# A three-pass state-space, attention and feed-forward kernel: areas, start-up loads and six splits rearranged at the borders of its passes

## The chip, the cores and the metric

The kernel runs on one core of one Trainium2 chip. A core has five engines that work from instruction queues of their own, each in order: TensorE (PE, matrix products into PSUM), VectorE (DVE), ScalarE (ACT), GpSimd (POOL) and SyncE (SP, which here only issues DMAs). They share an on-chip memory (SBUF) and meet through semaphores; DMA engines move data between SBUF and device memory.

The metric is device time in microseconds (us). Before the change it is 9731.19 us, the median of three runs (9729.94 to 9732.88).

## The reference, cut to what matters

The input is an image batch of 8 x 64 x 64 x 96 in float32. The layer is computed in three stages, each with a residual sum:

```
# layer 0: group norm, then a selective scan in four directions
xin, z = split(group_norm(x) @ in_proj_w.T)            # 96 -> 192 + 192
xc     = silu(depthwise_conv3x3(xin) + conv_b)          # 192 channels, 64 x 64
xs     = [xc by rows, xc by columns, and both reversed] # K = 4 directions, length 4096
dts, B, C = split(x_proj_weight[k] @ xs[k])             # 6 + 16 + 16 rows
delta  = softplus(dt_projs_weight[k] @ dts + dt_projs_bias[k])
h      = h * exp(delta * A) + (delta * u) * B           # step by step, 16 states a channel
y      = sum_n(h * C) + D * u
out    = (layer_norm(y of 4 directions summed) * gamma + beta) * silu(z) @ out_proj_w.T
x      = x + out
# layer 1: attention without a softmax, on the 4096 tokens of an image
t = t + (q k^T / sqrt(16)) v @ Wff + bff                # of layer_norm(t), 6 heads
# feed-forward in float8 products with float16 sums
t = t + W2(relu(W1(layer_norm(t))))
```

The inner state has 192 channels, 16 states for each, 4 directions, 8 images and 4096 steps. Almost all of the time is in the scan over these.

## The kernel before, in words

**Three passes.** `pass1` (line 295) makes the group norm, the in-projection, the 3 x 3 convolution and silu, writes the convolved channels `u` to device memory by rows and by columns (`u_d`), and makes the x-projections (`xd_d`: dts, B and C in rows). `pass2` (line 569) runs the selective scan. `pass3` (line 961) adds up the four directions, does the layer norm and gate, out-projection, attention and feed-forward, and writes the output.

**The order of work is planned.** In each pass, work is written as small generators ("units") that yield before each step what engine it needs, an estimated cost and what must have been done. `weave` (line 169) simulates the engines with these estimates and issues the steps in the order that comes out; so a changed buffer, cost or condition can reorder instructions on an engine. `InOrder` (line 85) issues each instruction through one helper, and pins the order on that engine, which is why nearly all instructions of the profile show line 93. `Slots` (line 132) stands for buffers taken in turn, the next one only when the one that has been out longest is free; `Buffers` (line 151) for buffers of which the first free one is taken.

**Pass 1** handles the images in four pairs. 192 channels of two images are three blocks of 128 partitions, in the order (0, 2, 1): `convolution(pair, c)` (line 468) does nine taps on VectorE over a padded image `xpad` of 4096 elements a partition (one `tensor_scalar`, eight `scalar_tensor_tensor`), silu on ScalarE in two halves, four copies on ScalarE that turn rows into columns (`ut`, 1024 elements each) with two or three stores after each, and a store of `u` itself. Then `x_projection` (line 518), in pieces of 512 columns, and `split` (line 265).

**A split** makes three bfloat16 parts of float32 rows, so that later products can be done in bfloat16: one load `bq` from `xd_d`, a cast on ScalarE, a subtraction on GpSimd, a second cast, a second subtraction, and two stores. An image has two row orders (orientations) with three splits each: two for B (`b_d`) and one for dt (`dt_d`). `LATE = 5` (line 59): images 0 to 4 are split in pass 1, images 5 to 7 in pass 2 among the scans (`late_split`, line 722). `LATE_X = 7`: image 7's x-projections are late as well.

**Pass 2** has 192 pieces: 4 pairs x 3 blocks of channels x 4 directions x 4 pieces of 1024 steps. A piece loads `xdt` (dt rows), `xb` (B rows) and `u`, issued by GpSimd for the first piece and by SyncE later; delta = softplus of a product on TensorE; `da` = exp(delta a) on ScalarE, 16 of them; `du` = delta u on GpSimd; B times du for each state by TensorE broadcast and VectorE multiply, or by ScalarE (`x`) or GpSimd (`xg`) and TensorE transpose, in a PSUM tile `wide`; 16 scans `h` on VectorE; h times C on GpSimd (`c`, in eight multiplications of 2048 elements); and a sum over the states on TensorE into `acc`, which ScalarE copies to `y` and SyncE stores to `y_d` (`store_y`, line 916).

**Pass 3** works through 64 units of 512 tokens, eight an image. `load` (line 1064) brings `y`, `yo` (the two row orders), `zs` (silu of z, in two) and `xr`: five DMAs, all on SyncE. `first_part` (line 1078) adds `y` and `yo` on GpSimd, takes the layer norm (statistics `mvy` on VectorE and ScalarE), scales by gamma and beta (`gb`) into the gate `gt` on ScalarE, multiplies by `zs` on GpSimd, and adds the out-projection to `xr` as `t` on VectorE. Ahead of all units stand the parameter loads and four float8 weights, each loaded into one shared raw buffer (`load_quantized`, line 1021) and cast on VectorE.

**Areas.** Each pass opens pools of SBUF over the space that the pass before has left. A pool that is laid over old ones waits for their users; in the program this shows as semaphore waits on the first tile of the new pool.

Of the kernel before, what the change touches and what calls it, by code (L numbers as in the profile page):

```python
# [42 lines left out]
P = 128  # L43
# [7 lines left out]
T = 1024  # L51
# [7 lines left out]
LATE = 5  # L59
# [205 lines left out]
def split(engines, pool_of, cost, landing, src, row, rows, pieces, at, dst):  # L265
# [4 lines left out]
    bq = pool_of.tile([P, wide], F32, name="bq", tag="late2")  # L270
# [3 lines left out]
    bs = pool_of.tile([P, NS, wide], BF16, name="bs", tag="late")  # L274
# [20 lines left out]
def pass1(ctx, tc, g, load_dt_w, ident, mhalf, engines, w_xp, u_d, z_d, xd_d, b_d, dt_d):  # L295
# [5 lines left out]
    us_p = ctx.enter_context(tc.tile_pool(name="p1u", bufs=UB))  # L301
# [3 lines left out]
    ps_tr = ctx.enter_context(tc.tile_pool(name="p1tr", bufs=2, space=PSUM))  # L305
    ps_mm = ctx.enter_context(tc.tile_pool(name="p1mm", bufs=3, space=PSUM))
    ps_px = ctx.enter_context(tc.tile_pool(name="p1px", bufs=3, space=PSUM))
# [40 lines left out]
    xpad = [wp.tile([P, HH + 2, WW + 2], F32, name=f"xpad{c}") for c in range(4)]  # L348
    for t in xpad:
        pool.memset(t[:, 0, :], 0.0)  # L350
        pool.memset(t[:, HH + 1, :], 0.0)
        pool.memset(t[:, 1 : HH + 1, 0:1], 0.0)
        pool.memset(t[:, 1 : HH + 1, WW + 1 : WW + 2], 0.0)

    sts, gms, us, done = {}, {}, {}, {}
    pts, mms, pxs = Slots(2), Slots(3), Slots(3)
# [7 lines left out]
    def transposed(pool_of, name, b, q):  # L364
# [4 lines left out]
        pt = ps_tr.tile([P, GRP], F32, name="pt", tag="pt")  # L369
# [19 lines left out]
    def group_norm(b):  # L389
# [6 lines left out]
        pm, slot = ps_mm.tile([P, GRP], F32, name="pm", tag="mm"), mms.taken  # L396
# [9 lines left out]
        pv, slot = ps_mm.tile([P, GRP], F32, name="pv", tag="mm"), mms.taken  # L406
# [12 lines left out]
    def projection(b, q):  # L419
# [19 lines left out]
        xn = four.tile([C, GRP], F32, name="xn")  # L439
        act.activation(xn, pt[0:C, :], AF.Identity, bias=gms[b][:, 0:1], scale=gms[b][:, 1:2])  # L440
        def product(w):
            yield "pe", 0.75, 0.4, mms
            p = ps_mm.tile([P, GRP], F32, name="pa", tag="mm")
# [24 lines left out]
    def convolution(pair, c):  # L468
# [17 lines left out]
        for tap in range(9):  # L486
            end = yield "dve", 2.6 if tap == 0 else 4.4, 0.0
            if tap == 0:
                u = us_p.tile([P, L], F32, name="u")
# [16 lines left out]
        for w in (slice(i, i + WW // 4) for i in range(0, WW, WW // 4)):  # L506
            yield "act", 2.1
            ut = two.tile([P, L // 4], F32, name="ut")
            act.copy(ut.rearrange("p (w h) -> p h w", h=HH), uv[:, :, w])
# [8 lines left out]
    def x_projection(b, o, q):  # L518
# [4 lines left out]
        for ty, u in ((0, us[pair, j]), (1 + j, us[pair, 2])):  # L523
            end = yield ("pe", 0.62, 0.4) if px else ("pe", 0.62, 0.4, pxs)
            if px is None:
                px, slot = ps_px.tile([P, GRP], F32, name="px", tag="px"), pxs.taken
# [23 lines left out]
    for pair in range(NB // 2):  # L550
# [7 lines left out]
        for b in batches:  # L558
            for o in range(2 if b < LATE_X else 0):
                units += [("xproj", x_projection(b, o, q)) for q in range(NG)]  # L560
                if b < LATE:
                    units += [("split", after(("xd", b, o), split((act, pool, sp), two, 4.4, 4.0, xd_d[b][o], *w))) for w in splits(b, o, b_d, dt_d)]
# [6 lines left out]
def pass2(ctx, tc, g, ident, engines, fixed, w_xp, u_d, xd_d, b_d, dt_d, y_d):  # L569
# [5 lines left out]
    two = ctx.enter_context(tc.tile_pool(name="p2two", bufs=2))  # L575
# [686 lines left out]
```

## Time and profile before

| what | value |
| --- | --- |
| median of three runs | 9731.19 us |
| profiled execution, its own time | 9730.31 us |
| span from first to last instruction in it | 9728.5 us |
| last convolution tap ends | 643.7 us |
| first scan starts | 682.91 us |
| last scan ends | 9049.0 us |
| first load of pass 3 issued | 9064.69 us |
| granted TensorE clock, mean | 0.976 |

The median stands 2.7 us over the span of the profiled execution, and 0.9 us over that execution's own time. Times are from the span's start. Engines appear as PE, PEld (weight loads), DVE, ACT, POOL and SP; SPq is the issuing of DMAs on SP. In a group of instructions, a name is written "output <- inputs", with the number of partitions and elements, and after a bar the busy time in us, the mean ns of one, and the engine's idle time just before them with what ended it. In a timeline a row is: start, duration of the row's instructions together, engine, line, operation, and in brackets how long the engine had been idle and what released it; instructions of one kind that follow closely stand in one row (x8).

### The profile page before, as it was taken

To read this page: it belongs to the slowest core of one execution; us is meant where nothing else is said; L and a number is where in the kernel's file an instruction comes from. 1 tells how busy PE (TensorE), PEld (TensorE's weight loads), DVE (VectorE), ACT (ScalarE), POOL (GpSimd) and SP (SyncE) were. 2 spreads that over 40 slices of the span, in tenths; PEclk is the share of its full clock that TensorE was granted. 3 is DMA by queue.
4 is the path that set the end of the run, shared out by engine and by line. 5 is a ranking of instruction groups with operands and counts; after the bars stand their busy time and mean duration, and the time that the engine had idled before them with its cause. 6 is when DMAs were issued, how large, how long until landed. Compare 5 with 4: busy or idle time off the path is not lost.

```text
span 9728.5 us, 163465 instructions
## 1 busy us (share of the span) xinstructions
PE 7918.3 (81%) x57248; PEld 6124.2 (63%) x57248; DVE 9305.7 (96%) x6971; ACT 9101.3 (94%) x21486; POOL 8996.0 (92%) x2911
## 2 busy tenths in 40 slices
PE   7868888888888888888888888888888888888787
PEld 3336666666666666666666666666666666666676
DVE  7879999999999999999999999999999999999788
ACT  5769999999999999999999999999999999999797
POOL 1449999999999999999999999999999999999777
PEclk8889999999999999999999999999999999999998
DMA  5777776789986777799976767899867767999763
GB/s 165 235 225 229 233 236 226 242 221 213 217 225 221 236 228 227 233 212 211 214 227 225 232 219 227 229 209 213 223 221 233 225 220 230 219 210 216 198 184 108
DMA packets 939446, 2120.78 MB, mean 218 GB/s; under 512 B 277676, under 2 KB 425933, under 8 KB 937091
## 3 DMA queue, kind: packets, MB, share of 16 engines
q1 hardware_dynamic: 935818, 2108.97, 77.6%
q8 instruction: 458, 7.50, 0.3%
q14 instruction: 362, 2.96, 0.1%
q0 software_dynamic: 432, 0.94, 0.0%
q10 hardware_dynamic: 2376, 0.40, 0.0%
HBM read 1934.36 MB, written 175.66 MB: 217 GB/s over the span
## 4 chain that ended last, share of the span: by engine, by line
ACT 31%; DVE 26%; issue 18%; POOL 10%; PE 10%; DMA 4%; SPq 1%; DVEq 0%; POOLq 0%; ACTq 0%
DVE h L93 20%; ACT x L93 13%; ACT da L93 11%; POOL c L93 8%; PE wide L93 3%; DVE wide L93 3%; PE acc L93 2%; ACT y L93 1%; PE px L93 1%; PE pa L93 1%; DMA c<-xd_d 1%; ACT L93 1%; ACT duT L93 1%; ACT delta L93 1%; PE mm L93 1%
## 5 line engine op out<-in xcount | busy, mean ns | idle before, releaser
L93 POOL TENSOR_TENSOR c<-c,h 128x2048 f32<-128x2048 f32 x1536 | 6961.4, 4561 | 80.5 <-DVE h L93 54.1
L93 DVE TENSOR_TENSOR_SCAN h<-da,carry,wide 128x1024 f32<-128x1024 f32 x2304 | 5242.4, 2328 | 72.9 <-PE wide L93 37.3
L93 ACT ACTIVATE x<-duT,bT 128x128 f32<-128x128 f32 (+1 forms) x14336 | 4229.4, 368 | 2.1
L93 ACT ACTIVATE da<-delta,a_neg 128x1024 f32<-128x1024 f32 x3072 | 3507.1, 1145 | 182.5 <-DVE h L93 173.6
L93 PE MATMUL acc<-ident,c 128*128 128x128 f32 x24576 | 3123.7, 276 | 340.2 <-POOL c L93 332.2
L93 PEld LDWEIGHTS acc<-ident,c 128*128 128x128 f32 x24576 | 2753.0, 141 | 783.5 <-POOL c L93 670.7
L93 PE MATMUL wide<-ident,x 128*128 128x128 f32 x11264 | 1496.9, 277 | 427.6 <-DVE h L93 326.5
L93 DVE TENSOR_TENSOR_SCAN h<-da,wide 128x1024 f32<-128x1024 f32 x768 | 1704.6, 2268 | 37.0 <-PE wide L93 24.8
L93 PEld LDWEIGHTS wide<-ident,x 128*128 128x128 f32 x11264 | 1246.5, 141 | 697.5 <-DVE h L93 181.7
L93 DVE TENSOR_TENSOR wide<-du,wide 128x1024 f32<-128x1024 f32 x1216 | 1457.0, 1209 | 51.1 <-issue 25.5
L93 PE MATMUL acc<-sel,zero 96*128 96x512 bf16 x4096 | 1131.4, 381 | 0.0
L93 PE MATMUL wide<-xb,sel 96*128 96x512 bf16 x2432 | 722.8, 381 | 295.2 <-DVE h L93 265.6
L93 POOL TENSOR_TENSOR xg<-duT,bT 128x512 f32<-128x512 f32 (+1 forms) x640 | 896.2, 1417 | 4.8 <-ACT duT L93 4.8
L93 PE MATMUL wide<-ident,xg 128*128 128x128 f32 x3584 | 487.5, 280 | 162.8 <-DVE h L93 148.2
L93 PEld LDWEIGHTS <-zero 96*128 96x128 bf16 x4096 | 398.4, 98 | 319.3 <-issue 6.3
L93 PEld LDWEIGHTS wide<-ident,xg 128*128 128x128 f32 x3584 | 404.5, 143 | 256.5 <-issue 204.5
L93 PEld LDWEIGHTS <-sel 96*128 96x128 bf16 x2432 | 221.0, 98 | 493.1 <-issue 294.9
L93 POOL TENSOR_TENSOR du<-delta,u 128x1024 f32<-128x1024 f32 x192 | 458.4, 2388 | 16.7 <-DMA u<-u_d 9.5
L93 DVE SCALAR_TENSOR_TENSOR u<-xpad,conv_w,u 128x4096 f32<-128x4096 f32 x96 | 451.5, 4704 | 1.9
L93 PE MATMUL wide<-ident,du 128*128 128x128 f32 x1536 | 205.1, 277 | 85.4 <-DVE h L93 68.2
L93 POOL TENSOR_TENSOR bq<-bq,bs 128x512 f32<-128x512 f32 (+1 forms) x48 | 122.0, 2544 | 163.3 <-ACT bs L93 147.6
L93 ACT ACT_TABLE_LOAD x196 | 251.5, 1283 | 17.0 <-DMA b2q_raw<-in_b 13.5
(150 smaller groups left out, 6171.5 us busy)
## 6 DMA issues: line engine op xcount, KB each, us to landing
c<-xd_d SPq DMA_DIRECT2D x1024, 1024.0 KB
c<-xd_d SPq DMA_DIRECT2D x1024, 512.0 KB
u<-u_d SPq DMA_DIRECT2D x127, 512.0 KB
xdt<-dt_d SPq DMA_DIRECT2D x1146, 36.0 KB
xb<-b_d SPq DMA_DIRECT2D x382, 96.0 KB
u<-u_d SPq DMA_DIRECT2D x128, 256.0 KB
zs<-z_d SPq DMA_DIRECT2D x128, 256.0 KB
y_d<-y SPq DMA_DIRECT2D x96, 256.0 KB
```

What stands on the lines that cost most here:

```text
L93: ins = getattr(self.engine, op)(*args, **kwargs).ins
```

## The change

- `LATE` goes from 5 to 4: image 4's six splits are made among the scans of pass 2.
- In pass 1, the PSUM tiles and the `u` tiles get a buffer by name (`tag`), and the PSUM buffers are taken first free (`Buffers`) instead of in turn (`Slots`). `xpad` is laid in the order 0, 2, 3, 1.
- In the last convolution, block 1 of pair 3, the turned copies are made on VectorE: two of 1024 elements and four of 512, in place of four of 1024 on ScalarE.
- In pass 2, the pools are laid in a new order. The buffers of even and odd pieces have pools of their own. The last piece's `y` store is issued by ScalarE.
- In pass 3, the units 0, 1 and 2 are to be loaded first; then gamma, beta and `w_out`; later the other weights, each float8 one in a raw buffer of its own and cast after all are loaded; GpSimd's fills of the `ln` tiles after the second sum of `y` and `yo`. Buffers are taken first free here as well.

```diff
-LATE = 5
+LATE = 4
...
 def split(engines, pools, cost, landing, src, row, rows, pieces, at, dst):
-    bq = pool_of.tile([P, wide], F32, name="bq", tag="late2")
+    bq = pools[0].tile([P, wide], F32, name="bq", tag="narrow")
-    bs = pool_of.tile([P, NS, wide], BF16, name="bs", tag="late")
+    bs = pools[1].tile([P, NS, wide], BF16, name="bs", tag="wide")
...
 # pass 1
-    xpad = [wp.tile([P, HH + 2, WW + 2], F32, name=f"xpad{c}") for c in range(4)]
+    xpad = {c: wp.tile([P, HH + 2, WW + 2], F32, name=f"xpad{c}") for c in (0, 2, 3, 1)}
-    pts, mms, pxs = Slots(2), Slots(3), Slots(3)
+    pts, mms, pxs = Buffers(2), Buffers(3), Buffers(3)
-        pt = ps_tr.tile([P, GRP], F32, name="pt", tag="pt")
+        pt = ps_tr.tile([P, GRP], F32, name="pt", tag=f"pt{pts.taken}")
...
-        for w in (slice(i, i + WW // 4) for i in range(0, WW, WW // 4)):
-            yield "act", 2.1
-            ut = two.tile([P, L // 4], F32, name="ut")
-            act.copy(ut.rearrange("p (w h) -> p h w", h=HH), uv[:, :, w])
+        last = (pair, c) == (NB // 2 - 1, ORDER[-1])
+        for i in range(6 if last else 4):
+            wide = WW // 8 if last and i > 1 else WW // 4
+            w0 = i * wide + (WW // 4 if last and i > 1 else 0)
+            w = slice(w0, w0 + wide)
+            yield ("dve", wide * 0.07) if last else ("act", 2.1)
+            if wide == WW // 4:
+                ut = two.tile([P, L // 4], F32, name="ut")
+            else:
+                ut = four.tile([P, L // 8], F32, name="ut8", tag="xn")
+            (dve.tensor_copy if last else act.copy)(ut.rearrange("p (w h) -> p h w", h=HH), uv[:, :, w])
...
 # pass 2
+    half[0], y0_p, delta_p, pools["xg"] = pool_of("even"), pool_of("y0"), pool_of("delta"), pool_of("xg")
+    one, wide_late, y1_p, late_p = pool_of("one"), pool_of("late4"), pool_of("y1"), pool_of("late2")
+    pools["da"], pools["x"], pools["h"], half[1], pools["c"] = pool_of("da"), pool_of("x"), pool_of("h"), pool_of("odd"), pool_of("c")
...
         if k >= 2:
-            yield "sp", 3.0, 6.0
-            store_y(ys[o], o, of, chunk_rows(pair, c))
+            end = at == len(pieces) - 1
+            yield ("act", 0.4) if end else ("sp", 3.0, 6.0)
+            store_y(act if end else sp, ys[o], o, of, chunk_rows(pair, c))
...
 # pass 3
+    LOADED, HELD, EARLY = 5, 20, 3
+    first_w, loaded = pool_of("first"), pool_of("loaded")
+    wp, one, each, gates, held = (pool_of(name) for name in ("w", "one", "each", "gates", "held"))
...
+    def parameters():
+        yield "load", 0, EARLY - 1
+        end = yield "sp", 2.0, 2.5
+        for i, name in enumerate(("ln_gamma", "ln_beta")):
+            sp.dma_start(gb[:, 0, i : i + 1], g[name][0:P].unsqueeze(1))
+            sp.dma_start(gb[:, 1, i : i + 1], g[name][DI - P : DI].unsqueeze(1))
+        sp.dma_start(w_out0, g["out_proj_wT"][0:P, :])
+        sp.dma_start(w_out1[64:P], g["out_proj_wT"][P:DI, :])
+        done[("gamma",)] = end
+        yield "load", 0, LOADED - 1
...
+            raw = one.tile(list(q.shape), F32, name=f"raw{len(quantized)}")
+            sp.dma_start(raw[0 : src.shape[0]], src)
+            quantized.append((q, raw, src.shape[0]))
+        yield "dve", 1.8
...
+    def fills():
+        yield "added", 1
...
     def load(b, q):
+        end = yield "sp", 0.0 if b == 0 and q < EARLY else 7.0, 2.5, slots["loaded"]
...
     def first_part(b, q):
+        if b * UNITS + q < OPEN:
+            yield ("gamma",)
...
-    weave(units, {"load": 1, "first": OPEN, "attention": 1, "second": OPEN}, done)
+    weave(units, {"parameters": 1, "fills": 1, "load": 1, "first": OPEN, "attention": 1, "second": OPEN}, done)
```

## The prediction

> **What bounds the kernel now.** I first read the busy shares and the costliest groups, to see where the time lies:
>
> ```profile
> PE 7918.3 (81%) x57248; PEld 6124.2 (63%) x57248; DVE 9305.7 (96%) x6971; ACT 9101.3 (94%) x21486; POOL 8996.0 (92%) x2911
> ...
> L93 POOL TENSOR_TENSOR c<-c,h 128x2048 f32<-128x2048 f32 x1536 | 6961.4, 4561 | 80.5 <-DVE h L93 54.1
> L93 DVE TENSOR_TENSOR_SCAN h<-da,carry,wide 128x1024 f32<-128x1024 f32 x2304 | 5242.4, 2328 | 72.9 <-PE wide L93 37.3
> ```
>
> The scan pass holds both. A table by windows then tells the passes and their borders apart (columns: window, its length, busy us of PE, PEld, DVE, ACT, POOL with counts, granted clock, DMA share, GB/s):
>
> ```profile
> 650.00:675.00 25.00, 3.28 (x19) 2.37 (x20) 0.55 (x3) 14.59 (x10) 8.27 (x12) 0.50 0.89 257
> 690.00:9050.00 8360.00, 6892.97 (x51676) 5433.10 (x51677) 8222.59 (x4284) 8114.59 (x19542) 8273.25 (x2401) 0.99 0.81 224
> 9050.00:9075.00 25.00, 6.72 (x45) 4.50 (x43) 6.34 (x29) 2.60 (x3) 10.11 (x18) 0.74 0.45 115
> 9075.00:9100.00 25.00, 17.15 (x72) 13.87 (x72) 8.94 (x53) 14.66 (x31) 13.40 (x9) 0.58 1.09 336
> ```
>
> Inside the scan pass POOL and DVE are about 99% busy: any POOL work added there costs time. The two borders are nearly empty: that is what can be won. At the first border, timelines of DVE, ACT and POOL:
>
> ```profile
> 603.71 40.01 DVE L93 SCALAR_TENSOR_TENSOR u<-xpad,conv_w,u 128x4096 f32<-128x4096 f32 x8
> 682.91 4.46 DVE L93 TENSOR_TENSOR_SCAN h<-da,wide 128x1024 f32<-128x1024 f32 x2
> ```
> ```profile
> 651.43 3.89 ACT L93 ACTIVATE u<-u,conv_b 128x2048 f32<-128x2048 f32 x2
> 670.90 1.91 ACT L93 COPY ut<-u 128x1024 f32<-128x1024 f32 x1 [0.60 <-DMA u_d<-ut]
> ```
> ```profile
> 657.79 1.15 POOL L93 TENSOR_TENSOR bs<-bq,bs 96x512 bf16<-96x512 f32 x1 [5.04 <-ACT bs L93]
> 658.89 3.28 POOL L93 DMA_DIRECT2D xdt<-dt_d  x6
> ```
>
> From the last tap (643.7) to the first scan DVE computes nothing but 0.59 us of constants: 39.2 us. POOL issues the first scan loads only after image 4's last subtraction, 658.89; I call this T0. At the second border, SP, ACT and DVE:
>
> ```profile
> 9064.69 0.42 SPq L93 DMA_DIRECT2D y<-y_d  x1
> 9078.88 0.78 ACT L93 ACTIVATE gt<-tr,gb 128x512 f32<-128x512 f32 x1 [0.57 <-PE tr L93]
> 9087.33 0.56 DVE L93 TENSOR_TENSOR t<-mm,xr 128x384 f32<-128x384 f32 x1 [4.99 <-DMA zs<-z_d]
> ```
>
> The last scan ends at 9049.0, the first load goes out 15.7 us later, and only from about 9107 is ACT (6 us a unit) full. It idles 26.2 us between 9059.8 and there.
>
> **What the Trainium skill says.** "SBUF — State Buffer", section "SBUF: two separate sides": GpSimd and VectorE share one port pair, held for a whole instruction. The trace agrees in kind: a tap has a mean of 4.47 us without a split beside it and 4.97 in the last convolution, with seven subtractions beside it; a subtraction takes 2.54 us there and 1.19 in the scan pass. The same section warns that a DMA issued by GpSimd cannot write its descriptors while VectorE makes an fp32 copy in SBUF; no row of this trace shows that. "VectorE: DVE Perf Modes", section "The perf-mode tier table", gives such a copy double rate; the trace has it for a neighbour, the first tap, 4096 elements in 2.35 us. "DMA: Bandwidth & Descriptors", section "Issuing engines are not separate DMA queues": another issuing engine saves only issue time.
>
> **The change, part by part.**
>
> *First border.* Removed ahead of it: image 4's six splits. Those in the last convolution cost its eight taps 8 x (4.97 - 4.47) = 4.0 us, so the taps end at 639.7. ACT then has only the remaining x-projection copies (0.58 us each, which end near 643) ahead of two silu halves, 3.9 us. They end at S = 647.5 or so, against 655.3. I allow 644 to 652, for the x-projections depend on the new order of the PSUM buffers. In the new program's waits, POOL's first loads stand no longer behind a split but behind the second silu half, since the pool for even pieces lies over `conv_w`, `conv_b` and `xpad0`. So T0 becomes S + 0.5 = 648.
>
> From T0, before: the u load at +8.6 (667.49), the delta product at +10.6 (669.48), the product of u for `acc` at +14.2 (673.10, 3.75 us), the first multiply at +21.7 and the first scan at +24.0. ACT's last two turned copies (668.37 and 670.90) and a table load held delta to +15.2. Without them delta is done by +15.1 at most and du follows (2.34 us) to +17.4. PE then transposes du as its `acc` product ends, +17.9, rather than +18.8; multiply +20.8, scan +23.1, or 671. The new waits that could come after: the first scan and `da` lie over u's area and wait for the landing of u's last store, 2 MB; it goes out behind the turned stores, and at the border's 257 GB/s takes about 8 us, landing near +19: hidden by 2 to 4 us.
>
> The moved copies: 6 on DVE, from 0.6 us (double rate, an estimate from the table of the skill) to 1.12 (full rate) per 1024 elements, 2.4 to 4.5 us, in DVE's idle gap: nothing. On ACT, 7.7 us go. But they run beside POOL's six descriptors; if these starve, T0's loads slip by up to 4.5 us. I take a gain of 682.9 - 671.1 = **-11.8 us**, bounded by -17 (S = 644 and copies at once) and -4 (S = 652 and starved descriptors).
>
> *Splits among the scans.* 12 subtractions of 1.19 us on POOL, 12 casts of 0.61 us on ACT (7.3 us, in ACT's 3% of slack), 6 loads and 12 stores on SP, which has slack. In the new order of instructions three more splits stand in block 1 of pair 1, one in its block 2 and two in block 0 of pair 2; all others stay where they are. What one costs the trace shows, by the starts of the `y` copies on ACT: in pair 1, with a split about every second or third piece, a piece takes 43.0 us on average, in pairs 2 and 3 without splits 42.5 to 42.7, which comes to about 1.1 us for a split in blocks 0 and 1; block 2 is bound by POOL alone (44.7 to 45.0 us a piece), so the full 2.37 us can show. 5 x 1.1 + 2.0 = **+7.5 us**; ends 2 (DVE bound, POOL's slack takes it) and 14.2 (all POOL time).
>
> *Rest of pass 1.* First-free PSUM buffers reorder PE, ACT and SP from about 225 us on. Of DVE's waits before 645 us, 48.9 us are for the statistics' transposes and 31.1 (four, up to 11.7) for ACT's `xpad` writes. Either sign: **0**, bounds -16 and +6.
>
> *Second border.* The idea is: loads first. But in the new program the first `y` load waits for all four of the last `y` stores to land: pool `loaded` overlaps the area of `y1` by 3.3 KB a partition. ACT copies y at 9058.8 to 9059.8, issues four stores (some 0.6 us each from the row of SP before, to 9062.3), and they land about 4 us later; so the first load leaves near 9066.5, 1.8 us later than before. The first sum may then come 1.8 later or, without weights between the loads, with the second sum at 9076 rather than 9078.3. Gamma now stands behind four units' loads, 20 DMAs of about 0.92 us (a unit took 4.3 to 4.9 us from 9074 on), then six of 0.45: it lands near 9066.5 + 18.4 + 2.7 = 9087.6, say 9088, while `gt` ran at 9078.9 before. ACT and DVE are in order: behind that `gt` wait further norms on ACT, and DVE's sums and statistics for them; behind the casts of the raw weights (landed about 9099.5) waits the first `t`. Against that, 3 to 5 units are loaded when gamma arrives, and ACT can then run without gaps, at 6 us a unit. Counting unit by unit, at 9113 the new order is 0.8 us behind the old: **+0.5**, bounds -12 and +10. The fills (3 us POOL) and the last raw casts lie in idle time.
>
> *Sum:* -11.8 + 7.5 + 0 + 0.5 = -3.8. Against the profiled execution: span 9728.5 - 3.8 = 9724.7, its own time 9726.5; the median of the runs stands 2.7 over the span: **9727 us**.
>
> **The rivals.**
>
> *A, the loads-first start works.* If DMAs issued back to back are quicker than 0.92 us (a unit took 4.0 us in the first two loads), gamma lands by 9082 and ACT is full from there: of its 26.2 idle us some 12 go. For it: DMA share is only 0.45 until 9075. Against: 1.09 after. -3.8 - 11.5 gives 9716.
>
> *B, pass 1 tightens.* A third of the 48.9 us of statistics waits goes through first-free buffers: -16, 9711. For it: they are the largest waits of DVE there. Against: most lie at the very start, before the order changes.
>
> *C, slower than before: gamma too late.* One mechanism: all of pass 3 waits at the first `gt` for six small DMAs behind twenty large. Each us after 9092 costs one us at the end, and from 9095.8 it eats the whole 3.8. At 1.3 us a DMA (the slowest unit before took 6.5 us for five) it lands near 9066.5 + 33.8 = 9100: +8.5, 9736. For it: that rate was seen as the queues filled. Against: those were units with a buffer to wait for.
>
> *D, nothing comes of the first border* (descriptors starve, S late): -4 instead of -11.8, 9735; it joins the forecast's upper end.
>
> **How the numbers follow.** Forecast 0.55 (own range 9717 to 9737, D included), A 0.20, B 0.13, C 0.12. What a measurement of this kernel can tell from no change is 0.2%, 19.5 us: below 9711.7 or above 9750.7. Faster: half of B and a little more (0.08), a third of A (0.07), where both come together or the borders gain all they can (0.06): 0.21. Slower: C at 1.9 us a DMA or worse, or with bad splits: 0.05. The range 9707 to 9741 holds C's and B's middles and leaves about one in ten at each side.
>
> **What would show it.** First scan at 671 (668 to 679), its POOL loads right behind the second silu half; about a us more for each of the six splits at its piece; first load of pass 3 at 9066 plus the shift, waiting for `y_d` stores; first `gt` some 22 us behind it; from then on ACT without long gaps. Wrong: a first scan later than 679 (starved descriptors), pass 1's last tap beyond 639.7 by more than 4 us either way, `gt` later than 27 us after the first load, or the scan pass longer by over 12 us.

## The result and the profile after

The changed kernel takes 9744.17 us (median of 20 runs, 9739.46 to 9753.30) against 9731.47 us before (20 runs, 9723.85 to 9742.91): a ratio of 1.0014, 95% interval 1.0007 to 1.0021. It is slower by 12.7 us, where 9727 and a range of 9707 to 9741 were forecast. Its profiled execution took 9741.95 us, its span is 9740.2 us, the granted clock 0.976.

The profile of the changed kernel; its busy shares and the two costliest groups:

```profile
PE 7929.9 (81%) x57252; PEld 6128.1 (63%) x57252; DVE 9290.4 (95%) x6977; ACT 9094.0 (93%) x21482; POOL 8958.7 (92%) x2911
...
L93 POOL TENSOR_TENSOR c<-c,h 128x2048 f32<-128x2048 f32 x1536 | 6965.3, 4567 | 64.9 <-DVE h L93 44.7
L93 DVE TENSOR_TENSOR_SCAN h<-da,carry,wide 128x1024 f32<-128x1024 f32 x2304 | 5244.4, 2331 | 68.6 <-PE wide L93 28.4
```

No engine but TensorE (PE 11.6 us longer of 7918.3, PEld 3.9) is busy for longer than before: the time has gone into waits. The table by windows shows where (columns as before: window, length, busy us of PE, PEld, DVE, ACT, POOL, clock, DMA share, GB/s):

```profile
650.00:675.00 25.00, 0.00 (x0) 0.00 (x0) 4.08 (x9) 4.95 (x4) 7.74 (x9) 0.57 0.58 207
690.00:9050.00 8360.00, 6885.79 (x51666) 5422.33 (x51666) 8227.04 (x4287) 8126.80 (x19575) 8284.54 (x2413) 0.99 0.80 224
9050.00:9075.00 25.00, 10.88 (x77) 7.82 (x75) 4.80 (x19) 1.01 (x1) 12.21 (x4) 0.84 0.24 70
9075.00:9100.00 25.00, 8.54 (x26) 4.89 (x26) 9.63 (x51) 13.18 (x27) 13.77 (x23) 0.50 0.94 277
```

Between 650 and 675 us PE now has nothing at all. The scan pass ends 5.2 us later; between 9050 and 9075 us ScalarE and VectorE do less than before, and from there to 9100 PE does half as much. The first border in timelines of DVE, ACT, SP and POOL:

```profile
608.50 36.91 DVE L93 SCALAR_TENSOR_TENSOR u<-xpad,conv_w,u 128x4096 f32<-128x4096 f32 x8
663.16 3.71 DVE L93 COPY ut<-u 128x1024 f32<-128x1024 f32 x6 [17.75 <-ACT u L93]
691.29 4.46 DVE L93 TENSOR_TENSOR_SCAN h<-da,wide 128x1024 f32<-128x1024 f32 x2
```
```profile
657.23 0.58 ACT L93 COPY xd<-px 76x512 f32<-76x512 f32 x1 [10.42 <-DMA xd_d<-xd]
658.76 0.58 ACT L93 COPY xd<-px 76x512 f32<-76x512 f32 x1 [0.94 <-DMA xd_d<-xd]
659.24 3.89 ACT L93 ACTIVATE u<-u,conv_b 128x2048 f32<-128x2048 f32 x2
```
```profile
639.57 2.50 SPq L93 DMA_DIRECT2D u_d<-u  x2
642.16 17.45 SPq L93 DMA_DIRECT2D xd_d<-xd  x6
```
```profile
663.43 6.15 POOL L93 DMA_DIRECT2D xdt<-dt_d  x6 [53.95 <-ACT u L93]
```

The last tap ends at 645.4 instead of 643.7. ScalarE then stands 10.4 us for a buffer of the x-projections, whose store SyncE issues behind two stores of u, 1 MB each; silu comes at 659.2, not 651.4; GpSimd's first loads follow it; its six `xdt` descriptors take 6.15 us instead of 3.28; the first scan starts at 691.3, not 682.9. At the second border, SP, ACT and DVE:

```profile
9069.69 0.38 SPq L93 DMA_DIRECT2D y<-y_d  x1
9091.20 0.78 ACT L93 ACTIVATE gt<-tr,gb 128x512 f32<-128x512 f32 x1 [1.43 <-PE tr L93]
9104.01 0.56 DVE L93 TENSOR_TENSOR t<-mm,xr 128x384 f32<-128x384 f32 x1 [0.44 <-PE mm L93]
```

From the last scan's end, at 9054.2, the first load is 15.5 us away (15.7 before), the first gate 37.0 (29.9), the first `t` 49.9 (38.3), the kernel's end 686.0 (679.5). By this pair of profiles: 8.4 us lost to the first scan, 3.2 won in the scan pass, 6.5 lost in the third pass.

That sum misleads, as the runs showed. Executions of one kernel lie up to 30 us apart (49 of the kernel before in one comparison: 9715.6 to 9745.4), the longer ones in part at a lower granted clock: in another comparison, the four at 0.978 lie at 9719 to 9727, the five at 0.974 at 9734.6 to 9738.9. The third pass of an unchanged source took from 679.1 to 689.2 us in five profiles, the scan pass with the same splits from 8357.5 to 8373.9 in fourteen. So an edit is judged below by medians of 7 to 21 runs, each against the kernel before in the same comparison. From the scatter of these runs such a difference has a standard error of 1.2 to 2.4 us (an estimate); the 95% intervals printed with the ratios are wider, 6 to 11 us either way. Two versions whose differences lie less than some 5 us apart are not told apart. A profile is used for a stretch only where several kernels agree on it.

### The profile page after: what moved, and what is told of

It reads as the page before. It is cut to its first block, busy times and chain, and to the rows that moved or that the text cites. A ratio compares the mean times of both kernels' runs of the same rounds, so it can differ in the third digit from the quotient of the medians.

```text
span 9740.2 us, 163459 instructions
## 1 busy us (share of the span) xinstructions
PE 7929.9 (81%) x57252; PEld 6128.1 (63%) x57252; DVE 9290.4 (95%) x6977; ACT 9094.0 (93%) x21482; POOL 8958.7 (92%) x2911
## 4 chain that ended last, share of the span: by engine, by line
ACT 33%; DVE 23%; issue 17%; POOL 10%; PE 7%; DMA 4%; SPq 1%; DVEq 0%; POOLq 0%; ACTq 0%
DVE h L93 19%; ACT x L93 14%; ACT da L93 12%; POOL c L93 8%; PE wide L93 3%; DVE wide L93 3%; PE acc L93 2%; DMA c<-xd_d 2%; ACT L93 1%; ACT y L93 1%; ACT delta L93 1%; ACT duT L93 1%; POOL xg L93 1%; DMA xd_d<-xd 1%; PE mm L93 1%
## 5 line engine op out<-in xcount | busy, mean ns | idle before, releaser
L93 ACT ACT_TABLE_LOAD x196 | 251.5, 1283 | 32.1 <-PE wide L93 15.6
L93 PE MATMUL px<-u,w_xp 128*128 128x512 f32 x448 | 221.8, 637 | 41.6 <-ACT u L93 31.8
```

The source lines that it names most:

```text
L93: ins = getattr(self.engine, op)(*args, **kwargs).ins
```

## The experiments

In the results, "over" and "under before" mean the kernel's median less that of the kernel before on the same chip. The changed kernel itself is 12.7 over. Of an experiment's edit the core is shown.

**Which pass loses it: the third passes exchanged.**

```diff
 # p3_new: the kernel before, with the changed kernel's pass3
-def pass3(...):   # of before
+def pass3(...):   # of after
 # p3_old: the changed kernel, with pass3 of the kernel before
```

> Passes 1 and 2 as before the change, pass 3 as after it. Theory (both borders cost: the first scan is 8.4 us late and the third pass takes 686.0 us from the last scan's end instead of 679.5): pass 3 is again some 6 us longer, first gate 36 to 38 us behind the last scan's end instead of 29.9, and the median lies 5 to 8 us over the kernel before. Rival (the longer third pass is only the scatter of one profiled run, all comes from the first border): third pass 679 to 681 us, median within 2 us of before.

Measured: 9721.98 us, 9.7 under before (ratio 0.9992, interval 0.9984 to 1.0000). Both expectations fell: the new third pass is no loss, and by the median a gain, though the interval just reaches no change. On the old passes it starts at once, since y1 does not lie under its loads there. From the SP timeline of this kernel, whose last scan ends at 9051.19:

```profile
9051.33 0.38 SPq L93 DMA_DIRECT2D y<-y_d  x1
```

Its profiled execution, 9733.3 us, was the slowest of its 13, so the length of its third pass is not compared.

> Passes 1 and 2 as after the change, pass 3 as before it. The new third pass alone gained about 10 us on the old passes (9722 against 9731.7), so the changed kernel's 12.5 us of loss come from passes 1 and 2 or from what they do to the third. Theory A (an interaction: the new place of y1 under the loaded units takes the new third pass's gain away; passes 1 and 2 themselves lose only the 4 us seen at the last scan's end): third pass 677 to 681 us as before, median 9733 to 9738. Theory B (the sum of parts: passes 1 and 2 lose 22 us and the new third pass gains 10 here too): median 9750 to 9756.

Measured: 9746.63 us, 16.0 over before (ratio 1.0015, 1.0009 to 1.0022); first scan at 691.8, third pass 679.1. Neither theory as it stood: the new passes 1 and 2 lose 16 us, more than A had; the new third pass gains 3 us on them, where it gained 10 on the old ones, less than B had. So the loss lies in the first two passes. That some 6 us of the third pass's gain are lost to what they leave behind is likely but not shown: the 3 us are within the scatter.

**The store order at the first border.**

```diff
         done["conv", pair, c] = end
...
+        if (pair, c) == (NB // 2 - 1, 2):
+            yield "xproj", 2 * pair
         end = yield "sp", 0.5
         for part, b, ch in parts:
             sp.dma_start(u_d[b][0][ch, :], u[part, :])
```

> The changed kernel, with the two 1 MB stores of u of the block before the last behind the x-projections' stores of image 6 on SyncE, where they stood before the change. Theory (the last silu stands on ScalarE behind x-projection copies that wait for buffers, whose stores are held behind those 2 MB): the last x-projection copy runs near 649 rather than 658.8, silu starts near 650 rather than 659.2, the first scan comes 6 to 10 us earlier, near 683, and the median falls by as much. Rival (the bytes have to pass anyway, and now hold the turned stores and the first loads instead): silu earlier, but first scan still at 689 or later, median within 2 us of the changed kernel.

Measured: last x-projection copy at 648.1, silu at 648.6, first scan at 684.0 (-7.3), as the theory has it; the median, 9740.94, is 9.2 over before (ratio 1.0009, 1.0001 to 1.0017), only 3.5 better than the changed kernel, which is within the scatter. Silu was won by 10.7 us and the first scan by 7.3: from silu to the first scan now took 35.5 us, not 32.1. The bytes go on to hold what comes next.

**Image 4's splits in pass 1 again**, in the changed kernel.

```diff
-LATE = 4
+LATE = 5
```

> The changed kernel, with image 4 split in pass 1 again (LATE = 5). Theory (the splits cost some 7 us among the scans, and the late first scan comes from the new order on SyncE, where u's 2 MB stay ahead): scan pass 4 to 8 us shorter, first scan at 693 to 700 since image 4's last splits now stand behind the last silu, median within 5 us of the changed kernel. Rival (moving the splits out of pass 1 is itself what brought the new order and the loss): first scan back at 683 to 686 and the median 8 to 12 us under the changed kernel.

Measured: 9751.19 us (7 runs), 20.6 over before (ratio 1.0025, 1.0014 to 1.0036); first scan at 700.6. The rival is out: under the new arrangement the splits in pass 1 are worse, by 7.9 us against the changed kernel. That is more than the 5 us that the theory had, too, and the scan pass, 8367.1 us, was not shorter in this one profile.

**The last turned copies on ScalarE again**, in the changed kernel.

```diff
-        last = (pair, c) == (NB // 2 - 1, ORDER[-1])
+        last = False
```

> The changed kernel, with the last turned copies on ScalarE again, four of 1024. Theory (beside VectorE's copies GpSimd wrote its six first descriptors in 6.15 us instead of 3.28, and the copies hold nothing else): xdt issue 3.3 us again, but ScalarE has 7.7 us of copies and waits for their two buffers ahead of delta, as before; first scan at 688 to 692, median within 3 us of the changed kernel. Rival (the slowed descriptors are what makes the first scan late): first scan at 684 to 687.

Measured: 9741.55 us, 10.9 over before (ratio 1.0012, 1.0005 to 1.0018): 1.8 better than the changed kernel, no more than the uncertainty; the first scan at 687.4 lies between the two bands, 3.9 earlier. GpSimd issues its six loads quickly again (6.2 us in all seven profiles with VectorE's copies beside them, 3.3 in the other eleven), and a wait shows that was hidden. From the POOL and ACT timelines of this kernel:

```profile
663.98 3.28 POOL L93 DMA_DIRECT2D xdt<-dt_d  x6 [53.84 <-ACT u L93]
```
```profile
674.89 1.11 ACT L93 ACTIVATE delta<-wide,dt_b 128x1024 f32<-128x1024 f32 x1
682.45 1.28 ACT L93 ACT_TABLE_LOAD   x1 [6.45 <-DMA u_d<-u]
```

Between delta and the first `da`, ScalarE waits 6.45 us until the last 2 MB of u have landed, because the new pool for `da` lies over u. So both arrangements cost: with the copies on ScalarE, `da` waits for u's landing; with the copies on VectorE the loads are slow. In the changed kernel `da` has no such wait, but delta comes at 680.0 instead of 674.9, and the load of u, issued at 670.6, was there for PE at 683.9, 13.3 us later; with copies on ScalarE 6.8 us (668.3 to 675.1). VectorE's six copies are done in 3.7 us, and SyncE has sent off 2 MB of turned copies and 2 MB of u by 668.8, ahead of this load; with copies on ScalarE the store of u goes out at 674.0, behind it. That the stores are what delays the load is read from this order; it was not tried by itself.

**The start of the third pass**, in the changed kernel.

```diff
 # gamma_first
     def parameters():
-        yield "load", 0, EARLY - 1
         end = yield "sp", 2.0, 2.5
 # loads_clear
-    first_w, loaded = pool_of("first"), pool_of("loaded")
-    wp, one, each, gates, held = (pool_of(name) for name in ("w", "one", "each", "gates", "held"))
+    loaded, held, first_w = pool_of("loaded"), pool_of("held"), pool_of("first")
+    wp, one, each, gates = (pool_of(name) for name in ("w", "one", "each", "gates"))
 # clear_gamma: gamma_first's edit, and
     first_w, loaded = pool_of("first"), pool_of("loaded")
-    wp, one, each, gates, held = (pool_of(name) for name in ("w", "one", "each", "gates", "held"))
+    held, wp, one, each, gates = (pool_of(name) for name in ("held", "w", "one", "each", "gates"))
-    lns = [first_w.tile([P, NU, P], F32, name=f"ln{i}") for i in range(OPEN)]
+    lns = [wp.tile([P, NU, P], F32, name=f"ln{i}") for i in range(OPEN)]
```

> The changed kernel, with the six DMAs of gamma, beta and w_out issued ahead of the units' loads instead of behind four of them. The first load still waits for the last y stores. Theory (the late gamma costs the third pass its 6.5 us): first gate about 29 us behind the last scan's end instead of 37.0, third pass 679 to 681 us instead of 686.0, median 5 to 7 us under the changed kernel. Rival (the casts of the raw weights on VectorE, on which the first sum t waits until 49 us behind the end, decide, wherever gamma is): first gate at 29, first t still at 47 to 50, third pass 684 to 686.

Measured: 9739.79 us, 8.1 over before (ratio 1.0010, 1.0002 to 1.0018), 4.6 better than the changed kernel, yet the first gate is still 35.9 us behind the last scan, not 29. Gamma had held it for 1 us at most. ScalarE's timeline of this kernel:

```profile
9082.38 0.30 ACT L93 ACTIVATE mvy<-mvy,eps 128x4 f32<-128x4 f32 x1 [3.75 <-DVE mvy L93]
9082.70 1.86 ACT L93 ACTIVATE y<-y,mvy 128x192 f32<-128x192 f32 x4
9086.93 0.30 ACT L93 ACTIVATE mvy<-mvy,eps 128x4 f32<-128x4 f32 x1 [2.37 <-DVE mvy L93]
9087.25 1.86 ACT L93 ACTIVATE y<-y,mvy 128x192 f32<-128x192 f32 x4
9089.02 0.76 ACT L93 ACTIVATE gt<-tr,gb 128x512 f32<-128x512 f32 x1
```

In ScalarE's order the first gate stands behind the roots of the second and third units' variances, and these follow their loads. The first `t` came at 45.0 rather than 49.9, earlier than the rival's 47 to 50. The profile, the fastest execution of its 13, has 675.6 us for the third pass.

> The changed kernel, with the third pass's pools in another order, so that its loaded units lie over areas that are free before the last y stores (loaded, then held, then the rest). Theory (the overlap of 3.3 KB with y1 holds the first load 15.5 us): first load within 2 us of the last scan's end, first gate some 22 us behind it, third pass 8 to 14 us shorter than 686, which would be less than before's 679.5. Rival (ScalarE's last copy of y, at 9.8 us behind the end, its stores, and the casts of the weights still hold the units): third pass 680 us or more.

Measured: 9740.35 us, 8.7 over before (ratio 1.0009, 1.0001 to 1.0017), 4.0 better than the changed kernel. First load 6.9 us behind the last scan, gate 31.7: of the theory's 13.5 us and more for the load 8.6 came, of its 15 for the gate 5.3. The profile, the second fastest of its 13, has 675.8 us for the third pass, in the theory's band. So y1 did hold the first load, but not alone; what held it for the other 6.9 us was not tried.

> The changed kernel, with gamma, beta and w_out first on SyncE in a small pool that is free before the last scan, and the loaded units over areas that do not meet y1. Theory (late loads and late gamma each hold the start of the third pass): gamma is issued at or before the last scan's end, first load within 5 us of it, first gate 18 to 24 us behind it (37.0 in the changed kernel), third pass 668 to 675 us, median 10 to 15 us under the changed kernel. Rival (the third pass is held later, by the raw weights' casts and by five buffers of loaded units, whatever the start): third pass 676 to 682, median 3 to 6 us under the changed kernel, like the two single edits.

Measured: 9738.16 us, 7.5 over before (ratio 1.0006, 1.0000 to 1.0013), 5.2 better than the changed kernel. Gamma went out 6.9 us behind the last scan, the first load 9.8, the first gate came at 33.2: none as early as the theory had it. The third pass in the profile, 674.8 us, is in the theory's band, the gain in the median in the rival's. All three mends give about the same, 4 to 5 us, within the scatter of one another. The timelines point to the order on ScalarE and the loads' rate as what then holds the start; no run tried these.

**LATE = 4 alone, on the kernel before.**

```diff
-LATE = 5
+LATE = 4
```

> The kernel before, with LATE = 4 alone: image 4's splits among the scans, nothing else changed. Its queue on SyncE puts the 2 MB of u ahead of the last six x-projection stores, as in the changed kernel. Theory (taking the splits away is what turns that order round, and holds silu): last x-projection copy at 656 to 660, silu near 659, first scan at 684 to 690 instead of 683 to 686, the six splits cost 2 to 5 us in the scan pass, median 4 to 10 us over before. Rival (the new pools and the copies on VectorE make the border late; the splits' removal shortens it as forecast): first scan at 671 to 679, median between 6 us under and 1 us over before.

Measured: 9727.24 us, 4.6 under before (ratio 0.9993, 0.9987 to 1.0000); first scan at 667.2, earlier than either band. This was the largest surprise, for the theory's wait is there and yet the border is early. DVE and ACT of this kernel:

```profile
598.30 36.13 DVE L93 SCALAR_TENSOR_TENSOR u<-xpad,conv_w,u 128x4096 f32<-128x4096 f32 x8
667.16 4.46 DVE L93 TENSOR_TENSOR_SCAN h<-da,wide 128x1024 f32<-128x1024 f32 x2
```
```profile
642.93 0.58 ACT L93 COPY xd<-px 76x512 f32<-76x512 f32 x1 [10.26 <-DMA xd_d<-xd]
644.94 3.89 ACT L93 ACTIVATE u<-u,conv_b 128x2048 f32<-128x2048 f32 x2
```

ScalarE loses its 10.3 us here as well, but the last tap ended at 634.4, some 11 us before the changed kernel's, and from silu to the first scan it is 22.2 us, not 32.1. So two things remained: something that makes pass 1 longer, and something between silu and the first scan.

**The third pass of `clear_gamma` on the kernel before, and all mends in the changed kernel.**

```diff
 # before_p3
-def pass3(...):   # of before
+def pass3(...):   # of clear_gamma
 # all_fixed: the changed kernel with the edits of u_store_last, copies_act and clear_gamma
```

> Passes 1 and 2 as before the change; the new third pass with gamma first in a small pool and the loaded units clear of y1, as in clear_gamma. Theory (the new third pass gains where neither y1 nor gamma holds it, and the losses lie in the first two passes): median 9714 to 9720, faster than before by 11 to 17 us, and 2 to 8 us under the new third pass as it was on the old passes (9722). Rival (gamma first brings nothing where the loads are early): 9721 to 9724.

Measured: 9718.98 us, 12.8 under before, ratio 0.9987, 0.9981 to 0.9994; third pass 676.0 us. As the theory has it, and here the interval is clear of no change; the 3 us more than `p3_new` are within the scatter. Its first load goes out 9.9 us behind the last scan, not at once as in `p3_new`.

> The changed kernel with all three mends: u's 2 MB behind the x-projection stores, the last turned copies on ScalarE, gamma first and the loaded units clear of y1. Theory (the three single gains of about 4.4, 2.8 and 8.5 us add): first scan at 679 to 683, median 9727 to 9733, level with before, since the splits among the scans still cost. Rival (the two mends at the first border take the same wait): first scan at 684 to 687, median 9733 to 9738.

Measured: 9729.81 us, 2.0 under before (ratio 0.9996, 0.9988 to 1.0004): the theory's median; first scan 683.5, just above its band. The single gains that it added up are 3.5, 1.8 and 5.2 us by the differences given above, 10.5 together; all at once brought 14.7. Each alone is hardly clear of the scatter; together they are.

**The PSUM buffers of pass 1.**

```diff
 # slots_back: the changed kernel, with
-    pts, mms, pxs = Buffers(2), Buffers(3), Buffers(3)
+    pts, mms, pxs = Slots(2), Slots(3), Slots(3)
-        pt = ps_tr.tile([P, GRP], F32, name="pt", tag=f"pt{pts.taken}")
+        pt = ps_tr.tile([P, GRP], F32, name="pt", tag="pt")
...
 # late4_free: LATE = 4 on the kernel before, and there the reverse
-    pts, mms, pxs = Slots(2), Slots(3), Slots(3)
+    pts, mms, pxs = Buffers(2), Buffers(3), Buffers(3)
 # late4_again: late4_only once more
```

> The changed kernel, with pass 1's PSUM buffers taken in turn again (Slots, and pools of two, three and three); all else as changed. LATE = 4 alone ended the last tap at 634.4 us, the changed kernels at 645 to 648. Theory (first-free PSUM buffers, which reorder ScalarE, SyncE and TensorE in pass 1, cost some 10 us there): last tap at 633 to 639, first scan 8 to 12 us before the changed kernel's 691, median 9733 to 9738. Rival (pass 1 scatters by that much from execution to execution, 643.7 and 649.4 for the kernel before, and 634.4 was luck): last tap at 643 to 650, median 9742 to 9747.

> The kernel before with LATE = 4 and with pass 1's PSUM buffers taken first free, nothing else. Theory (as above): last tap at 644 to 649, first scan at 676 to 682, median 8 to 12 us over LATE = 4 alone (9727), so 9735 to 9739. Rival: last tap and median as with LATE = 4 alone, within 3 us.

> LATE = 4 alone once more, for the scatter of its profile: theory (the early last tap belongs to the order) last tap at 632 to 638, first scan at 665 to 671; rival (luck) last tap at 641 to 649. Median near 9727 either way.

Measured: in turn again, the changed kernel falls to 9728.90, 0.9 under before (ratio 0.9999, 0.9991 to 1.0008), 13.6 better. First free, LATE = 4 alone rises to 9738.70, 8.9 over before (ratio 1.0005, 0.9996 to 1.0013), 14.1 worse than the mean of its two runs (4.6 and 5.9 under: `late4_again` gave 9723.86, ratio 0.9995, 0.9987 to 1.0003). The same choice costs 14 us in both directions; resampling the runs leaves each of the two between some 6 and 19 us (an estimate). The last tap: 635.2 in `late4_again`, so no luck; 649.6 in `late4_free`; but 643.1 in `slots_back`, in the rival's band, and its first scan at 687.8 is 3.5 us earlier only; its scan pass was the shortest of all profiles, 8357.5. So by the profiles `late4_free` has its loss in pass 1, while `slots_back` has only 3.5 of its 13.6 us ahead of the first scan, and the rest in passes that were not edited, where single profiles scatter as much.

VectorE's two largest waits up to 650 us (waiting, for what: us in total, times, longest), in `late4_again`, `late4_free`, `slots_back` and the changed kernel:

```profile
DVE st L93 <- PE pt L93: 49.3, 22, 18.0
DVE u L93 <- ACT xpad L93: 29.7, 4, 12.5
```
```profile
DVE st L93 <- PE pt L93: 59.7, 22, 17.1
DVE u L93 <- ACT xpad L93: 34.4, 4, 14.1
```
```profile
DVE st L93 <- PE pt L93: 56.3, 24, 17.6
DVE u L93 <- ACT xpad L93: 30.6, 4, 11.3
```
```profile
DVE st L93 <- PE pt L93: 56.6, 21, 17.0
DVE u L93 <- ACT xpad L93: 30.7, 4, 10.8
```

First free, the waits for the statistics' transposes (`pt`) grow by 10.4 us and those for `xpad` by 4.7: together 15.1, about the 14.3 by which the last tap is later. Between `slots_back` and the changed kernel they are the same.

One place in pass 1 where time goes is the eighth convolution. Its first tap, in `late4_again`, the changed kernel and `late4_free` in turn (DVE timelines):

```profile
408.54 2.35 DVE L93 TENSOR_SCALAR u<-xpad,conv_w 128x4096 f32<-128x4096 f32 x1 [3.06 <-ACT xpad L93]
```
```profile
416.66 2.35 DVE L93 TENSOR_SCALAR u<-xpad,conv_w 128x4096 f32<-128x4096 f32 x1 [10.81 <-ACT xpad L93]
```
```profile
420.01 2.35 DVE L93 TENSOR_SCALAR u<-xpad,conv_w 128x4096 f32<-128x4096 f32 x1 [14.12 <-ACT xpad L93]
```

The seventh had begun at 362.1, 359.3 and 362.5, so 11 us are lost from one to the next (the changed kernel wins some of it back at the eleventh, where its wait is 6.5 us and that of `late4_again` 12.5). VectorE waits for ScalarE's `xpad` copies, and ScalarE stands ahead of some of them (ACT of the changed kernel, then of `late4_again`):

```profile
383.65 0.62 ACT L93 CAST bs<-bq 128x512 bf16<-128x512 f32 x1 [9.11 <-DMA bq<-xd_d]
384.18 0.58 ACT L93 COPY xpad<-pa 128x512 f32<-128x512 f32 x1
```
```profile
372.54 0.58 ACT L93 COPY xpad<-pa 128x512 f32<-128x512 f32 x1
379.94 0.62 ACT L93 CAST bs<-bq 96x512 bf16<-96x512 f32 x1 [6.83 <-DMA bq<-xd_d]
```

A split's cast waits for its load, at the head of ScalarE's queue, with copies for the convolution behind it; in turn, one of these copies came just ahead of the cast. ScalarE gets past this wait 3.7 us later in the changed kernel and 7.1 in `late4_free` (387.1), of the 8.1 and 11.5 us by which the tap starts later. Over 200 to 640 us the casts wait 10.6 to 11.8 us for `bq` with LATE = 4 in turn (four profiles) and 22 to 32 us first free (five profiles). But `slots_back` is one of the four, with 10.8 us, and it ended its taps only 2.3 us before the changed kernel. So the cost of the choice is shown by the medians; through which wait it comes is not. That the casts' wait is the link was not tried by itself, and it is at most a part.

**Versions that beat both.**

```diff
 # late4_p3: the kernel before, with
-LATE = 5
+LATE = 4
-def pass3(...):   # of before
+def pass3(...):   # of clear_gamma
 # late4_p3_u: the same, and in pass1 the edit of u_store_last
+        if (pair, c) == (NB // 2 - 1, 2):
+            yield "xproj", 2 * pair
```

> LATE = 4 on the old passes 1 and 2, with the mended third pass (gamma first, loads clear of y1). Theory (the gains of 5 us at the first border, net of the splits, and 12 us in the third pass add): median 9712 to 9717, faster than both kernels and than the old passes with the same third pass (9719). Rival (they don't add): 9718 to 9722.

Measured: 9715.89 us, 13.9 under before (ratio 0.9984, 0.9978 to 0.9991), the theory's band. That is only 1.1 us further under before than `before_p3`, where 5 would be full addition: the two gains add in part or within the uncertainty.

> LATE = 4 on the old passes and the mended third pass, with u's 2 MB behind six of the last eight x-projection stores as well. In the changed kernel the same edit took silu 10.7 us forward, but the first scan only 7.3, and the median 3 us. Theory (silu is held by the store queue, and the loads behind it then by the 2 MB): last x-projection copy at 637 to 641 instead of 648, first scan 4 to 8 us earlier than 672, median 9710 to 9714. Rival (the 2 MB then hold the first loads for as long as they held silu): silu earlier, first scan still at 670 to 674, median 9714 to 9718.

Measured: 9714.97 us, 15.8 under before (ratio 0.9984, 0.9977 to 0.9991), 1.9 further than `late4_p3`, within the scatter. The last x-projection copy ran at 636.1, silu at 636.6, the first scan at 670.7 instead of 672.0: the rival. Where the 12 us went, SP and ACT of this kernel:

```profile
642.48 18.47 SPq L93 DMA_DIRECT2D u_d<-ut  x4
```
```profile
656.94 3.67 ACT L93 COPY ut<-u 128x1024 f32<-128x1024 f32 x2 [12.76 <-DMA u_d<-ut]
```

The wait for u's 2 MB has moved from ahead of silu to between the turned copies, almost whole.

## Why the prediction was wrong

By the pair of profiles, the changed kernel's span lies 15.5 us over the forecast 9724.7: the first scan comes 20.2 us after the forecast 671.1, the scan pass is 10.7 us shorter than forecast, the third pass 6.0 longer. Of the 20.2 us, 5.7 are the last tap (645.4, not 639.7), 9.9 the way from there to the end of silu (663.1, not 647.5), and 4.6 the way from silu to the scan. Two of the prediction's own signs of being wrong thus showed. The medians of the runs shift these shares, as follows.

**What failed most: "Rest of pass 1: 0, bounds -16 and +6".** Taking PSUM buffers first free cost 13.6 and 14.1 us, the same choice tried on two kernels. I had seen that the order changes from about 225 us on, and taken it to be as likely good as bad. The orders themselves might have told more: which load a cast waits for, and what is queued behind it on ScalarE. Rival B, the same edit as a gain, is refuted: the statistics waits, of which it saw a third go, grew from 49.3 to 59.7 us in `late4_free`. No rival had a loss at that place; the one that ended slower, C, named another. By which wait the cost comes stays open, since `slots_back` gained as much with its waits in pass 1 as in the changed kernel.

**Image 4's splits.** With LATE = 4 on the old passes the first scan came at 667.2, 672.5 and 672.0 in three profiles, against 682.9, 685.8 and 681.0 with LATE = 5: 12.6 us earlier on average. That is near the forecast 11.8 by accident: the forecast was for the whole new border, with the new pools and without ScalarE's turned copies, none of which is in these kernels. The last tap was earlier than forecast (634 to 637, not 639.7; the contention of the taps fell as forecast, 36.1 us for eight taps instead of 40.0, and convolutions before also began earlier). But "x-projection copies which end near 643", 3 us behind the last tap, missed SyncE's queue: taking splits out of it put u's 2 MB ahead of the last x-projection stores, ScalarE stood 10.3 us, and the copies ended 11 to 14 us behind the tap, in the changed kernel 14. Of a step that goes, what closes up behind it on each queue belongs in the count too.

**"From T0 ... scan +23.1".** In the changed kernel it took 27.9 us. From the start of silu to the first scan, where 27.5 us were forecast, it took 22.2 to 23.5 us on the old pools with LATE = 4 (four profiles), 27.6 with the new pools (one profile), and 30.8 to 33.6 with the copies on VectorE too (six profiles with u's stores in their place). That u's landing would be "hidden" held for the changed kernel; with the copies on ScalarE it showed, 6.45 us. What the Trainium skill says in "SBUF — State Buffer", section "SBUF: two separate sides", shows here in kind: six DMAs took GpSimd 6.15 us to issue beside VectorE's copies and 3.28 without. That part I had as a bound of up to 4.5; what I had not was that the quick copies bring all stores at once, ahead of the load of u, which then takes 13.3 us instead of 6.8. By medians this arrangement costs 7.1 us (`p3_old`, 16.0 over, less `late4_free`, 8.9 over), which includes the other layout changes of passes 1 and 2.

**The splits among the scans: too dear by more than half.** Three of them, between pieces 72 and 80, cost 3.3 to 3.8 us together in each of 14 profiles with LATE = 4 against four with LATE = 5: 1.2 us a split, near the 1.1 worked out. The other three, one of them in block 2, cost nothing that could be told from the scatter of DMA waits there, where 2 x 1.1 + 2.0 were forecast; all six together, over pieces 72 to 104, 3.0 us on average, where 7.5 (2 to 14.2) were forecast. The whole scan pass is on average as long with them as without, 8366.0 us. The term that failed most is "the full 2.37 us can show".

**The second border: times right, the reason wrong.** Forecast first load 15.5 to 17.5 us behind the last scan's end: 15.5. First gate at 39 (9088): 37.0; first `t` behind the raw weights, which were to land at 50.5 (9099.5): 49.9. By profiles the new third pass, where y1 holds it, takes 684 us on average (five, 681.2 to 688.2) against 683 (five of the old one, 679.1 to 689.2), by medians it gains 3 us; +0.5 was forecast, and all of these agree within the scatter. But the gate did not wait for gamma: with gamma first it came only 1 us sooner. There it waits in ScalarE's order behind three units' statistics. So C's mechanism was not at work. A's gain, 12 us, came near on the old passes alone: 9.7 us for the new third pass (first load at 0.1 us), 12.8 with it mended (9.9 us). That an early first load makes the gain is not shown, for `gamma_first`, with its first load at 15.6, is as good within the scatter as the mends that start earlier.

**The sum as it turned out**, by medians along one chain of kernels: LATE = 4, -5; first-free buffers, +14; new pools, VectorE's copies and the rest of passes 1 and 2, +7; the new third pass on these, -3. The +7 and the -3 are what is left between neighbours of the chain, so that the sum +13 must meet the measured +12.7 and is no check of the shares. The forecast had -3.8.

## What to carry to other kernels

An edit to a scheduler's inputs, such as a buffer rule, is not neutral because it has no sign: read in the new order what each in-order engine waits for and what stands behind it, for here loads waited for at the head of ScalarE's queue stood ahead of a convolution's copies, and the choice cost 14 us. Putting u's 2 MB of stores behind the small ones moved the wait, in one trial almost whole, in the other by a third; moving the copies to a faster engine brought their stores together, and the load behind them came late. With changes of a tenth of a per cent, exchange whole passes both ways first: two such runs said which half lost and that the other half did not, where one pair of profiles had 6.5 us of the loss in that other half.

## What was not expected of the hardware

SyncE's issue of a small store was slow right behind large ones: in the changed kernel the `xd_d` store just ahead of u's 2 MB took 0.33 us to issue, the four right behind 2.1 to 2.6 us each, the two after these 0.24. GpSimd needed about twice as long to issue its six `xdt` loads while VectorE copied float32 in SBUF (6.15 against 3.28 us): 2.9 us more, beside copies of 3.7. VectorE's copies of 4096 elements a partition in six pieces, turned from rows to columns, took 3.71 us: about 0.9 us per 1024 elements, between the 0.6 and 1.12 that the prediction had allowed. The length of a third pass with no edit of its own differs by up to 10 us from one profile to another (679.1 to 689.2 us).
